# Wq's second half on GpSimd's queue, and the opening of a perceiver kernel put in TensorE's order

## The chip, the core and the metric

The kernel runs on one core of one Trainium2 chip. A core has engines that each work through their own list of instructions in order and wait for one another by semaphores: TensorE (PE, with its weight loads listed as PEld), VectorE (DVE), ScalarE (ACT), GpSimd (POOL) and SyncE (SP), which only issues transfers. Transfers issued by SP, ACT and POOL are carried out by 16 DMA engines that the core's queues share. The metric is the device time of one execution in microseconds (us), lower being better.

## What is computed

Three layers run one after the other on x of 4 x 128 rows by 1024 columns: cross attention to 8192 context rows, causal self attention, and a gated feed-forward layer with 4-bit weights. Each is added to x, and each reads a layernorm of x. What bears on the change is the opening of the first layer:

```python
def _layernorm(x, axis=-1, eps=1e-05):
    m = jnp.mean(x, axis=axis, keepdims=True)
    v = jnp.var(x, axis=axis, keepdims=True)
    return (x - m) / jnp.sqrt(v + eps)
...
    q = (x @ Wq + bq).reshape(1, B * N, H, hd)
    kv = (cond @ Wkv + bkv).reshape(1, -1, 2, H, hd)
...
    q = _fq_sym(q, axis=-1)
    k = _fq_sym(k, axis=-1)
    v = _fq_sym(v, axis=2)
```

Here x is the layernorm of the input, `cond` the context, and `_fq_sym` rounds to 8 bits with a scale for each head (for v, for each column).

## The kernel before

**The opening: queries.** The 512 rows of x are four tiles of 128 rows (`t`). For each tile: x is loaded (`load_x_of_q`, line 259), normalised on DVE with a square root on ACT (`layernorm`, line 132: two statistics of 512 columns, a few tiny operations, and one operation over 1024 columns that writes `xn`), transposed on PE in eight blocks of 128 x 128 into two PSUM tiles (`transposes_of_x`, line 275), copied back by ACT (`copies_of_x`, line 284), and multiplied with Wq. Wq is used in two halves of 512 columns (`n`), each in eight row blocks (`k`) of 128 x 512 that `load_wq` (line 263) fetches. A step of `project_q` (line 289) is one such block against one tile; eight steps make a tile of 128 x 512 queries. PE does all four tiles for the first half, then all four for the second. Eight results of 128 x 512 are then quantised on DVE (`quantise_q`, line 296: add bq, maximum per head, scale, round to 16-bit integers), transposed by DMA from SP's queue (`transpose_q`, line 302) and spread into `qT` by ACT (`store_q`, line 306).

**The opening: weights for values.** Meanwhile the eight row blocks of Wkv for the values come in (`weight_raw`, line 229, 512 KB each) and are split into three parts, so that three matmuls in a reduced format give nearly full precision: a high part on ACT (`weight_hi`), a low part and a difference on DVE (`weight_lo`, lines 158 and 159), and a scaling of the low part on ACT (`weight_up`). The context's tiles of tokens are split in the same way (`load_tokens`, `tokens_hi`, `tokens_lo`), and `project` (line 336, matmuls at line 342) multiplies tokens and weights: 48 matmuls for each of 64 tiles. DVE joins the results (lines 356 and 357), and GpSimd's queue stores them (line 362).

**Buffers.** Wq's blocks share nine buffers (`bufs=NC + 1`). Eight hold the first half and one the first block of the second; block k of the second half takes the buffer of block k-1 of the first, so it cannot be loaded before the last tile has used that one. x's tiles and the tokens' tiles share two buffers (`c_raw`), and so tile 2 of x waits until tile 0 has been normalised, tile 3 until tile 1 has. There is one buffer for `xn`, and two for a raw block of Wkv.

**The order.** The opening's order is written out by hand: `do(step, fn, ...)` puts a call on an agenda (line 219), and `perform` (line 222) makes the calls sorted by `step`, without a scheduler. The numbers are about microseconds, but only their order counts; an engine's list, and a queue's, is what remains of the agenda for it. After the second token tile's first half the order of the value phase is left to a scheduler, up to tile 60 (`V_AUTO`, line 69); from there on it is written by hand again. In the value phase DVE also expands the 4-bit weights of the feed-forward layer, one `expand` (line 386) or two per tile.

**Queues before.** All loads of the opening are on SP's queue, in this order: x 0, Wq's first half with x 1 in between, x 2, x 3, bq, Wq's block 0 of the second half, two blocks of Wkv, and then, each held until its buffer is free, transposes of queries, blocks of Wkv, biases, two token tiles, and the other seven blocks of Wq's second half. GpSimd has nothing between the identity matrix at the start and the first store of values.

Of the kernel before, what the change touches and what calls it, by code (L numbers as in the profile page):

```python
# [41 lines left out]
ALU = mybir.AluOpType  # L42
# [4 lines left out]
P = 128  # L47
B, S, C = 4, 128, 1024
NT = B * S // P
# [37 lines left out]
def tile_perceiver(  # L87
# [26 lines left out]
    nc = tc.nc  # L114
# [14 lines left out]
    gu_d = dram.tile([2 * NI, P, NC, P], F32, name="gu_d")  # L129
    dn_d = dram.tile([2, NI // 2, P, 2, 512], F32, name="dn_d")  # L130

    def layernorm(pool, xt, xn):
        st = pool.tile([P, 2, nc.vector.BN_STATS_DIM], F32, name="ln_st", tag="ln_st", bufs=2)
        for i in range(2):
            nc.vector.bn_stats(st[:, i, :], xt[:, ts(i, 512)])
        mv = pool.tile([P, 2], F32, name="ln_mv", tag="ln_mv", bufs=2)
        nc.vector.bn_aggr(mv, st)
        rstd = pool.tile([P, 1], F32, name="ln_rstd", tag="ln_rstd", bufs=2)
        nc.vector.tensor_scalar_add(rstd, mv[:, 1:2], 1e-5)
        nc.scalar.activation(rstd, rstd, AF.Sqrt)  # L140
        nc.vector.reciprocal(rstd, rstd)
        nc.vector.tensor_scalar(xn, xt, mv[:, 0:1], rstd, ALU.subtract, ALU.mult)

    def split(src, hi, lo, df):

# [60 lines left out]
    q_t = q_s.enter_context(tc.tile_pool(name="q_t", bufs=2, side="right"))  # L206
# [12 lines left out]
    def do(step, fn, *args):  # L219
        agenda.append((step, len(agenda), fn, args))  # L220
# [35 lines left out]
    wq_src = xWq.rearrange("(k p) n -> p k n", p=P)  # L256
    xts, xns, xnTs, qps, qns, wqs, bqs, xpts = {}, {}, {}, {}, {}, {}, {}, {}

    def load_x_of_q(t):
        xts[t] = early.tile([P, C], F32, name=f"xt{t}", tag="c_raw")  # L260
        nc.sync.dma_start(out=xts[t], in_=x[ts(t, P), :])

    def load_wq(n, k):
        wqs[n, k] = q_w.tile([P, 512], F32, name=f"wq{n}_{k}", tag="wq", bufs=NC + 1)
        nc.sync.dma_start(out=wqs[n, k], in_=wq_src[:, k, ts(n, 512)])

    def load_bq():
        bqs[0] = early.tile([P, C], F32, name="bq", tag="c_l2", bufs=1)
# [1 line left out]

    def norm_of_x(t):
        xns[t] = early.tile([P, C], F32, name=f"xn{t}", tag="c_h2", bufs=1)
        layernorm(q_t, xts.pop(t), xns[t])

    def transposes_of_x(t):
        xn = xns.pop(t)
# [93 lines left out]
    shifts = kv_w.tile([P, 2], I32, name="shifts")  # L370
# [66 lines left out]
    def open_pool_of_v():  # L437
        q_s.close()
        pools["v"] = kv_only.enter_context(tc.tile_pool(name="kv_v", bufs=2))

    do(0, load_x_of_q, 0)
    for k in range(NC):
        do(0.1 if k < 3 else 0.3, load_wq, 0, k)
        do(0.6 if k == 0 else 34.6 + 0.88 * k, load_wq, 1, k)
    do(0.2, load_x_of_q, 1)
    for t in range(2, NT):
        do(0.4, load_x_of_q, t)
    do(0.5, load_bq)
    do(32, lambda: nc.sync.dma_start(out=shifts, in_=nibbles))
    do(0.5, nc.vector.memset, vmax, 0.0)  # L450
    for t, at in enumerate((4, 10.5, 20, 22.6)):
        do(at, norm_of_x, t)
        do(9 if t == 0 else 6.85 + 8.15 * t, transposes_of_x, t)
        do(9.1 if t == 0 else 6.95 + 8.15 * t, copies_of_x, t)
        for n in range(2):
            at = (10 + 8.15 * t, 42.6 + 7.05 * t)[n]
            for k in range(NC):
                do(at + 0.88 * k, project_q, n, t, k)
            do(at + 7.2, quantise_q, n, t)
            do(at + 10.7, transpose_q, n, t)  # L460
            do(at + 15, store_q, n, t)
    for k, at in enumerate((28, 30.5, 36.2, 38.7, 44.3, 46.8, 52.4, 54.9)):
        do(20 if k < 2 else at - 8, weight_raw, 1, k)
        do(at - 1.2, weight_hi, 1, k)
        do(at, weight_lo, 1, k)
        do(at + 2.5, weight_up, 1, k)
    for n in range(2):
        do(32, kv_bias, 1, n)
        do(32, load_tokens, n)
    do(58.2, tokens_hi, 0)  # L470
    do(59.4, tokens_lo, 0)
    do(62, load_tokens, 2)
    at = 70.8
    for s in range(2):
        for n in range(2):
            for k in range(NC):
# [163 lines left out]
    for s in range(V_AUTO, 2 * KT):  # L640
        at = TILE * s
# [8 lines left out]
    at = TILE * V_AUTO  # L650
# [11 lines left out]
    at = TILE * (KT - 2)  # L662
# [5 lines left out]
    at = TILE * KT  # L668
# [12 lines left out]
    for u in range(KT):  # L681
        at = TILE * (KT + u)
# [15 lines left out]
    at = TILE * (KT + 2)  # L698
# [4 lines left out]
    first, last = V_QUANT  # L703
    done = 0
    for u in range(first, last):
        at = TILE * (KT + u)
# [5 lines left out]
    at = TILE * (2 * KT - 1)  # L712
# [21 lines left out]
    with tc.tile_pool(name="at_e", bufs=1) as at_e, tc.tile_pool(  # L734
# [245 lines left out]
        with tc.manual_schedule():  # L980
            for s in range(n_steps + LAG_V):
                n, g = divmod(s, NSC)
# [9 lines left out]
                if n < len(units):  # L992
                    h, t = units[n]
# [316 lines left out]
    with tc.manual_schedule():  # L1310
# [10 lines left out]
        for h, (w, n) in enumerate(PARTS):  # L1321
            s = PART * h

            if h > 0:
                for kp in range(NC // 2):
                    at = s + {1: (-28, -24, -13.8, -10), 2: (-35, -31, -6, -3)}.get(h, (-26, -16, -6, -3))[kp]
# [69 lines left out]
        for i in range(2):  # L1396
            at = s - 26 + 10 * i
# [218 lines left out]
```

## Time and profile before

| | us |
|---|---|
| median of 3 runs | 2857.21 (2855.76 to 2858.63) |
| the profiled execution | 2854.13 |
| its span, first to last instruction | 2852.4 |
| PE busy in the span | 2652.6 (93%) |
| DVE busy | 2421.2 (85%) |
| ACT busy | 1267.0 (44%) |
| POOL busy | 455.7 (16%) |

The mean clock granted to TensorE was 0.987 of full speed. The chain of work that ended last goes through PE for 70% of the span and through DVE for 21%; by line, 32% and 16% are the keys-and-values matmuls of line 342, 14% an operation of the attention on DVE (line 789), and 2% the query projection (line 292).

In the rows of a profile, L12 is line 12 of the kernel; `out<-in` names the tiles; `x8` is the number of instructions merged into a row; what stands in brackets is how long the engine was idle just before, and what ended that. SPq is SP's issuing of transfers, whose times are those of issuing and not of moving data. A matmul of 32-bit numbers leaves two records. Rows of one engine can overlap a little, since matmuls are pipelined. DMA transfers end some time after they are issued; the profile gives that time as "to landing".

### The profile page before, as it was taken

The page shows a single profiled execution, that of the slowest core. Times are in us where ns is not written, and L with a number is a line of the kernel's source. Part 1 is how long each engine was busy: PE and PEld are TensorE (multiplying, and loading weights), DVE is VectorE, ACT ScalarE, POOL GpSimd, SP SyncE. Part 2 cuts the span into 40 slices and gives each one's busy share as a digit, 9 for nine tenths or more (in the row PEclk, how much of TensorE's full clock was granted, in tenths as well). Part 3 has the DMA queues.
Part 4 walks back from the last instruction along what each step waited for, and adds up shares of the span by engine and source line. Part 5 has one row for each costly group of instructions (what it writes and reads, how often), then busy time and mean ns, then how long its engine had stood idle before and what let it go on. Part 6 is the DMA issues. An engine that isn't in the chain of part 4 may idle for free.

```text
span 2852.4 us, 41096 instructions
## 1 busy us (share of the span) xinstructions
PE 2652.6 (93%) x15496; PEld 2059.5 (72%) x15496; DVE 2421.2 (85%) x3960; ACT 1267.0 (44%) x1404; POOL 455.7 (16%) x608
## 2 busy tenths in 40 slices
PE   8999999999999999999996777787778899999998
PEld 3788888888878888888884555555555777788886
DVE  6899999555699998888879999999997898876674
ACT  4211211112323333333217999999994244333332
POOL 0011111000012222222113332233312000000000
PEclk9999999999999999999998999999999999999999
DMA  5555565222447777777536888877875222122222
GB/s 188 170 200 201 194 212 207 104 96 95 146 106 198 192 192 186 188 186 191 130 88 144 164 167 165 154 149 161 164 145 153 76 83 67 52 96 96 94 92 96
DMA packets 450631, 412.66 MB, mean 145 GB/s; under 512 B 354872, under 2 KB 359544, under 8 KB 450432
## 3 DMA queue, kind: packets, MB, share of 16 engines
q1 hardware_dynamic: 402848, 251.70, 36.3%
q0 software_dynamic: 46528, 157.29, 17.2%
q8 instruction: 122, 2.00, 0.3%
q10 hardware_dynamic: 1056, 1.05, 0.2%
q14 instruction: 77, 0.63, 0.1%
HBM read 220.14 MB, written 104.34 MB: 114 GB/s over the span
## 4 chain that ended last, share of the span: by engine, by line
PE 70%; DVE 21%; issue 4%; POOL 2%; ACT 1%; DMA 1%; DVEq 0%; ACTq 0%
PE kv_a L342 32%; PE kv_b L342 16%; DVE e L789 14%; PE acc_a L1130 3%; PE up_a L165 3%; PE gate_a L165 3%; PE y_a L1503 3%; POOL sk L762 2%; PE q_ps L292 2%; PE acc_b L1130 1%; PE up_b L165 1%; PE gate_b L165 1%; PE y_b L1503 1%; PE a_pt L832 1%; DVE sw_l L158 1%
## 5 line engine op out<-in xcount | busy, mean ns | idle before, releaser
L342 PE MATMUL kv_b<-w_d,c_d 128*128 128x512 f32 x2048 | 806.0, 394 | 0.3 <-DVE c_d L159 0.3
L342 PE MATMUL kv_a<-w_h,c_h 128*128 128x512 f32 x2048 | 806.3, 394 | 0.0
L342 PE MATMUL kv_a<-w_l,c_l 128*128 128x512 f32 x2048 | 806.0, 394 | 0.2 <-ACT w_l L246 0.2
L789 DVE CUSTOM_DVE_ANT_0 e<-sc,sk 128x1024 f32<-128x1024 f32 x512 | 593.0, 1220 | 8.1 <-PE sc L782 7.0
L817 ACT ACTIVATE a<-e,m,sqs 128x4096 int16<-128x4096 f32 x128 | 486.9, 3804 | 24.1 <-DVE m L806 23.8
L342 PEld LDWEIGHTS kv_a<-w_l,c_l 128*128 128x128 f32 x2048 | 384.8, 188 | 89.6 <-ACT w_l L246 0.6
L342 PEld LDWEIGHTS kv_b<-w_d,c_d 128*128 128x128 f32 x2048 | 384.8, 188 | 89.5 <-DVE c_d L159 0.8
L342 PEld LDWEIGHTS kv_a<-w_h,c_h 128*128 128x128 f32 x2048 | 384.9, 188 | 88.8 <-issue 0.2
L155 ACT ACTIVATE c_h<-c_raw 128x1024 fp32r<-128x1024 f32 x128 | 135.2, 1057 | 418.9 <-PE kv_a L342 404.6
L356 DVE SCALAR_TENSOR_TENSOR f<-kv_a,bkv 128x512 f32<-128x512 f32 x256 | 175.8, 687 | 163.4 <-PE kv_a L342 162.8
L782 PE MATMUL sc<-kt,qT 64*128 64x512 bf16 x1024 | 205.5, 393 | 104.9 <-DVE mx L789 100.8
L581 ACT CAST kst<-kT 128x512 bf16<-128x512 int16 x128 | 89.4, 699 | 302.3 <-DMA kT<-ki 302.3
L832 PE MATMUL a_pt<-ident,a 128*128 128x128 f32 x1024 | 174.3, 295 | 21.1 <-ACT a L817 16.4
L357 DVE SCALAR_TENSOR_TENSOR f<-kv_b,f 128x512 f32<-128x512 f32 x256 | 176.7, 690 | 20.3 <-DVE f L356 0.9
L762 POOL PARTITION_BROADCAST sk<-sk_row x120 | 142.3, 1297 | 312.3 <-DVE mx L789 312.2
L832 PEld LDWEIGHTS a_pt<-ident,a 128*128 128x128 f32 x1024 | 111.4, 144 | 86.9 <-ACT a L817 48.9
L782 PEld LDWEIGHTS <-qT 64*128 64x128 bf16 x1024 | 75.3, 93 | 132.7 <-issue 102.7
L158 DVE TENSOR_TENSOR fw_l<-fw_raw,fw_h 128x1024 fp32r<-128x1024 f32 x64 | 78.3, 1224 | 99.4 <-ACT fw_h L155 99.3
L158 DVE TENSOR_TENSOR c_l<-c_raw,c_h 128x1024 fp32r<-128x1024 f32 x128 | 155.7, 1217 | 5.8 <-ACT c_h L155 5.6
L159 DVE SCALAR_TENSOR_TENSOR c_d<-c_l,c_raw 128x1024 fp32r<-128x1024 f32 x128 | 156.3, 1221 | 2.3
L155 ACT ACTIVATE fw_h<-fw_raw 128x1024 fp32r<-128x1024 f32 x64 | 67.8, 1060 | 175.4 <-PE y_a L1503 71.6
L548 ACT CAST vq<-vi 128x1024 f16<-128x1024 int16 x64 | 67.0, 1046 | 171.0 <-DVE vi L541 123.9
(211 smaller groups left out, 4104.9 us busy)
## 6 DMA issues: line engine op xcount, KB each, us to landing
c_raw<-in_ctxT SPq DMA_DIRECT2D x128, 512.0 KB, 3.6
v_d<-f POOLq DMA_DIRECT2D x64, 512.0 KB, 3.1
vl<-v_d POOLq DMA_DIRECT2D x64, 512.0 KB, 4.2
gu_d<-w_ffn POOLq DMA_DIRECT2D x44, 512.0 KB, 3.1
fw_raw<-gu_d SPq DMA_DIRECT2D x42, 512.0 KB, 3.2
k_d<-kst POOLq DMA_DIRECT2D x128, 128.0 KB, 3.5
vq_d<-vq POOLq DMA_DIRECT2D x32, 512.0 KB, 5.2
kt<-k_d SPq DMA_DIRECT2D x64, 256.0 KB, 3.5
```

What stands on the lines that cost most here:

```text
L155: nc.scalar.mul(hi, src, 1.0 - 0.5 / UP)
L158: nc.vector.tensor_tensor(lo, src, hi, ALU.subtract)
L159: nc.vector.scalar_tensor_tensor(df, lo, -1.0 - UP, src, ALU.mult, ALU.add)
L165: nc.tensor.matmul(ps, lhsT=lhs(i, k), rhs=rhs(i, k), start=(k == 0 and i != 1), stop=(k == NC - 1 and i != 0),)
L342: nc.tensor.matmul(ps, lhsT=tokens[s][i][:, k, :], rhs=w3[s < KT][k][i][:, ts(n, 512)], start=(k == 0 and i != 1), stop=(k == NC - 1 and i ...
L356: nc.vector.scalar_tensor_tensor(f, a, 1.0 + 1.0 / UP, bias[s < KT][n], ALU.mult, ALU.add)
L357: nc.vector.scalar_tensor_tensor(f, b, -1.0 / UP, f, ALU.mult, ALU.add)
L762: nc.gpsimd.partition_broadcast(tile_of_scales(h, g), sks_at[h][32 * c : 32 * c + 1, ts(half, SC)], channels=P)
L782: nc.tensor.matmul(ps[:, ts(i, 512)], lhsT=qT[rows, h, ts(t, P)], rhs=kts[h, g // 2][rows, ts(g % 2, 512)], start=True, stop=True,)
L789: nc.vector.tensor_tensor_reduce(out=state[n]["e"][-1][:, ts(g % (NSC // NEC), SC)], in0=ps, in1=sks_at[h, g], scale=1.0, scalar=LOWEST, o ...
L817: nc.scalar.activation(a, st["e"][c], AF.Exp, bias=st["m"], scale=sqs[:, 0, t, h : h + 1], accum_out=sums[h][:, t, c : c + 1],)
L832: nc.tensor.transpose(pt[:, i, :], a[:, at_word + P * i : at_word + P * i + P], ident)
```

## The change

`load_x_of_q` fetches tile 0 of x in two halves of 512 columns, and `layernorm` writes tile 0's `xn` in two operations of 512 columns. `load_wq` puts blocks 1 to 7 of the second half on GpSimd's queue instead of SP's. The agenda's numbers are new: two blocks of Wkv and bq move ahead of tiles 2 and 3 of x on SP's queue, the first two token tiles are loaded earlier, the biases later; PE takes seven steps of a tile, and not six, before the next tile's transposes; the layernorms, splits and quantisations are placed anew on DVE, with a quantisation no longer ahead of the next layernorm but behind it; ACT's conversions follow. The numbers of instructions stay, but for one more load of x and one more operation on DVE. With the hand-written part, the scheduler's order of DVE, ACT, POOL and SP in the value phase differs too, up to about its end; PE's list is the same from the second half of the queries on.

```diff
-    def layernorm(pool, xt, xn):
+    def layernorm(pool, xt, xn, parts=1):
...
-        nc.vector.tensor_scalar(xn, xt, mv[:, 0:1], rstd, ALU.subtract, ALU.mult)
+        for i in range(parts):
+            cols = ts(i, C // parts)
+            nc.vector.tensor_scalar(
+                xn[:, cols], xt[:, cols], mv[:, 0:1], rstd, ALU.subtract, ALU.mult
+            )
...
-        nc.sync.dma_start(out=xts[t], in_=x[ts(t, P), :])
+        for i in range(2 if t == 0 else 1):
+            cols = ts(i, 512) if t == 0 else slice(0, C)
+            nc.sync.dma_start(out=xts[t][:, cols], in_=x[ts(t, P), cols])
...
-        nc.sync.dma_start(out=wqs[n, k], in_=wq_src[:, k, ts(n, 512)])
+        queue = nc.gpsimd if n == 1 and k > 0 else nc.sync
+        queue.dma_start(out=wqs[n, k], in_=wq_src[:, k, ts(n, 512)])
...
-        layernorm(q_t, xts.pop(t), xns[t])
+        layernorm(q_t, xts.pop(t), xns[t], parts=2 if t == 0 else 1)
...
     do(0, load_x_of_q, 0)
     for k in range(NC):
         do(0.1 if k < 3 else 0.3, load_wq, 0, k)
-        do(0.6 if k == 0 else 34.6 + 0.88 * k, load_wq, 1, k)
+        do(0.65 if k == 0 else 30, load_wq, 1, k)
     do(0.2, load_x_of_q, 1)
-    for t in range(2, NT):
-        do(0.4, load_x_of_q, t)
-    do(0.5, load_bq)
-    do(32, lambda: nc.sync.dma_start(out=shifts, in_=nibbles))
+    do(0.45, load_bq)
+    do(0.5, load_x_of_q, 2)
+    do(0.55, load_x_of_q, 3)
     do(0.5, nc.vector.memset, vmax, 0.0)
-    for t, at in enumerate((4, 10.5, 20, 22.6)):
+    first = [8.1 + 8.05 * t for t in range(NT)]
+    second = [39.2 + 7.03 * t for t in range(NT)]
+    for t, at in enumerate((4, 9, 16.4, 24.5)):
         do(at, norm_of_x, t)
-        do(9 if t == 0 else 6.85 + 8.15 * t, transposes_of_x, t)
-        do(9.1 if t == 0 else 6.95 + 8.15 * t, copies_of_x, t)
-        for n in range(2):
-            at = (10 + 8.15 * t, 42.6 + 7.05 * t)[n]
+        at = first[t] - (1.6 if t == 0 else 1.9)
+        do(at, transposes_of_x, t)
+        do(at + 0.1, copies_of_x, t)
+        for n, q_at in enumerate(((19, 27.5, 33, 40.9)[t], (48.7, 54.1, 61, 67.5)[t])):
             for k in range(NC):
-                do(at + 0.88 * k, project_q, n, t, k)
-            do(at + 7.2, quantise_q, n, t)
-            do(at + 10.7, transpose_q, n, t)
-            do(at + 15, store_q, n, t)
-    for k, at in enumerate((28, 30.5, 36.2, 38.7, 44.3, 46.8, 52.4, 54.9)):
-        do(20 if k < 2 else at - 8, weight_raw, 1, k)
-        do(at - 1.2, weight_hi, 1, k)
-        do(at, weight_lo, 1, k)
-        do(at + 2.5, weight_up, 1, k)
+                do((first, second)[n][t] + 0.88 * k, project_q, n, t, k)
+            do(q_at, quantise_q, n, t)
+            do(q_at + 3.1, transpose_q, n, t)
+            do(q_at + 8.5, store_q, n, t)
+    for k, (raw, hi, lo) in enumerate(
+        (
+            (0.4, 12.8, 13),
+            (0.6, 19.5, 22),
+            (16.5, 24, 30.4),
+            (24.6, 34, 36),
+            (33, 37.5, 38.4),
+            (38.5, 42, 43.8),
+            (41, 49.5, 51.6),
+            (46.3, 55, 57),
+        )
+    ):
+        do(raw, weight_raw, 1, k)
+        do(hi, weight_hi, 1, k)
+        do(lo, weight_lo, 1, k)
+        do(lo + 2.6, weight_up, 1, k)
     for n in range(2):
-        do(32, kv_bias, 1, n)
-        do(32, load_tokens, n)
-    do(58.2, tokens_hi, 0)
-    do(59.4, tokens_lo, 0)
-    do(62, load_tokens, 2)
-    at = 70.8
+        do(27.6, load_tokens, n)
+        do(40, kv_bias, 1, n)
+    do(45, tokens_hi, 0)
+    do(46.2, tokens_lo, 0)
+    do(48.8, load_tokens, 2)
+    do(60, lambda: nc.sync.dma_start(out=shifts, in_=nibbles))
+    at = 67.4
```

## The prediction

> **What bounds it now.** I read the chain of waits first. Its shares by line say that TensorE's matmuls are the path: the projections of lines 342 and 292, then DVE in the attention. The change touches only the opening, so next came the busy time of 100 us stretches, to see whether a gain there survives. After the stretch come the columns its length, then busy time (instructions) of PE, PEld, DVE, ACT, POOL, then granted clock, DMA share, GB/s.
>
> ```profile
> 0.00:100.00 100.00, 87.31 (x263) 48.64 (x264) 66.32 (x126) 38.79 (x51) 1.42 (x7) 0.97 0.58 175
> 100.00:200.00 100.00, 100.00 (x434) 81.26 (x433) 100.00 (x220) 19.13 (x18) 14.32 (x25) 1.00 0.55 195
> ...
> 300.00:400.00 100.00, 100.00 (x434) 81.26 (x433) 98.61 (x196) 19.13 (x18) 16.42 (x26) 1.00 0.56 198
> ...
> 1200.00:1300.00 100.00, 100.00 (x434) 81.24 (x433) 89.78 (x139) 34.67 (x39) 22.31 (x34) 1.00 0.74 190
> ```
>
> PE misses 12.7 us in the first 100 us (7.88 before it begins, 0.85 and 3.96 below) and next to nothing until 1400 us. What starts earlier there shifts all that follows. So the question is where those 12.7 us lie. The timeline of PE over the opening answers it (start, length, operation, idle before it in brackets):
>
> ```profile
> 7.88 1.94 PE L281 MATMUL pt<-ident,xn 128*128 128x128 f32 x8 [7.88 <-DVE xn L142]
> 9.64 6.27 PE L292 MATMUL q_ps<-wq,xnT 128*128 128x512 f32 x12
> 15.75 1.04 PE L281 MATMUL pt<-ident,xn 128*128 128x128 f32 x8
> 16.62 7.03 PE L292 MATMUL q_ps<-wq,xnT 128*128 128x512 f32 x16
> 24.50 1.09 PE L281 MATMUL pt<-ident,xn 128*128 128x128 f32 x8 [0.85 <-DVE xn L142]
> 25.43 7.03 PE L292 MATMUL q_ps<-wq,xnT 128*128 128x512 f32 x16
> 32.30 1.04 PE L281 MATMUL pt<-ident,xn 128*128 128x128 f32 x8
> 33.18 9.61 PE L292 MATMUL q_ps<-wq,xnT 128*128 128x512 f32 x22
> 46.74 29.84 PE L292 MATMUL q_ps<-wq,xnT 128*128 128x512 f32 x62 [3.96 <-DMA wq<-in_xWq]
> 76.01 0.80 PE L342 MATMUL kv_a<-w_h,c_h 128*128 128x512 f32 x1
> ```
>
> A projection step is two records. Eight steps take 25.43 to 32.30, so 0.859 us each; a tile's eight transposes take 15.75 to 16.62, 0.87. From 16.62 there are 58 steps and two sets of transposes to the first keys-and-values matmul: 58 x 0.859 + 1.74 = 51.6, which would end at 68.2. It comes at 76.01, so 7.8 us are lost: 0.85 for xn of the third tile, 3.95 (42.79 to 46.74) for the second half of Wq, 2.64 after it (31 steps need 26.63, from 46.74 to 76.01 are 29.27), and 0.4 in small seams. The 2.64 are a slow clock and short waits:
>
> ```profile
> 44.00:48.00 4.00, 1.26 (x2) 0.50 (x2) 3.35 (x8) 1.06 (x1) 0.00 (x0) 0.69 1.19 312
> 48.00:52.00 4.00, 3.99 (x5) 1.46 (x5) 0.34 (x1) 2.42 (x4) 0.00 (x0) 0.50 0.97 341
> 52.00:56.00 4.00, 4.00 (x10) 1.71 (x9) 3.93 (x4) 1.98 (x2) 0.00 (x0) 0.96 0.51 173
> ```
>
> After the idle stretch TensorE was granted half its clock until about 52 us. Why did Wq come late? SP's queue:
>
> ```profile
> 36.53 1.53 SPq L323 DMA_DIRECT2D c_raw<-in_ctxT  x1
> ...
> 38.58 0.43 SPq L323 DMA_DIRECT2D c_raw<-in_ctxT  x1
> 39.11 0.37 SPq L265 DMA_DIRECT2D wq<-in_xWq  x1
> ```
>
> The load takes the buffer of Wq step 0, which tile 3 releases at 33.18 + 3 x 0.859 = 35.8. It is issued at 39.11, behind loads of Wkv, a transpose, two biases and two token tiles, and its matmul starts at 46.74: 3.3 us in the queue, 7.6 in transfers that share the engines with 1.5 MB issued just ahead.
>
> **The change, part by part.**
>
> Seven Wq loads go to GpSimd's queue. Nothing stands ahead of them there but the identity's making (over at 1.5 us), nothing behind but the first store of values, which is due after the first keys-and-values tile. Each waits for PE alone. With tile 3's step 0 done at 33.9 (below), the loads are released every 0.859 us, and load j is needed 6.9 us after its release, because seven more steps of tile 3 and one of the new half lie between. The trace of before has no Wq load on this queue. Nearest row: loads of vl from DRAM there, twice the size, 0.55 us to issue and 3.5/4.2/6.8 us to landing (min/median/max). At 4.2 from issue there are 2.7 us to spare, at 6.8 still 0.1. The low end, a smaller landing, changes nothing; the high end is 7.6 us, what Wq took on the crowded queue: 0.7 late. I take 4.2: the two token tiles that crowded it are issued by about 28 us here, and the biases after the sixth Wkv load, at about 39.
>
> Here a rule speaks against the change. The Trainium skill, "SBUF — State Buffer", section "SBUF: two separate sides", says that a transfer from GpSimd's queue has its descriptors written by GpSimd, which is locked out while DVE runs an operation in a two-port mode; its subsection "A bandwidth-pool intuition that's wrong (but worth ruling out)" prices one such case at 3100 ns instead of 620. By the rule, if every load met it, the seven would be generated at 3.1 us each: load 7 issued at 33.9 + 21.7 = 55.6, landed about 59, needed at 45.9, so 13 us of stall. By the row: while DVE is busy 100% (100 to 200 us), POOL issues its stores in 0.53 to 0.77 us, and stores of v_d land in 3.2. In the 8 us in question DVE runs quantisations and splits (1.22 us for 1024 columns, two inputs), not the 0.81 us normalisation, which looks like the fast mode and ends by 28 us. I take the row.
>
> SP loses those seven issues (0.33 to 0.95 us each, off its way), so Wkv's loads leave as soon as their buffers free. The 1 KB load of shifts moves behind them all; its user comes far later. The first two Wkv tiles move to the start of the queue, one of them and bq ahead of tiles 2 and 3 of x. By bytes: x 0.5, Wq 2.1, x 0.5, Wkv 0.5, bq 0.5, x 1.0 MB. The trace moved 0.84 MB by 5 us and 344 GB/s up to 9; continued at 370 that lands Wkv at 13, bq at 14.5, tile 2 of x at 16, tile 3 (held for its buffer to 12.6) at 18. ACT converts the first Wkv tile ahead of tile 1's copies, so a landing after 16 would hold up PE; there are 3 us between.
>
> DVE's order. With a layernorm of 3.0, a quantisation of 3.0 and a split of 2.45 us (sums of their rows), and PE as the pace: norm 1 to 12.6, split 0 to 16.5, norm 2 to 19.6 (PE wants it at 23.4; before it came at 24.45, behind a quantisation that waited for PE), quantisation to 22.6, split 1 to 25.1, norm 3 to 28.1 (wanted at 31.2). Five more quantisations, six splits of weights and one of tokens follow; the last weight is ready at 60.3, tokens at 49, and the keys need them at 67. DVE then waits for PE. The 0.85 goes, and no new wait takes its place: slack is 3 us at the norms, 7 at the weights. The quantisations' order does hold up ACT's stores and with them splits 4 to 7 (ACT waits for the transpose by DMA, 4.2 us), which is in these figures.
>
> The first norm by halves. x lands at 4.70 and two statistics of 0.68 follow. With two loads the first half should land about a microsecond earlier, and its statistics (0.64 by start-to-start) hide under the second's landing; 0 if the second half lands that much later (one issue later is 0.46), so 0.2 to 0.64. The 0.81 normalisation becomes two of about 0.44, and PE begins after the first: 0.37; DVE pays 0.07 more. I take 0.64 + 0.37 = 1.0, at worst 0.5. PE's cold start (1.94 for the first transposes, against 1.04) stays.
>
> Scheduler. From the second token tile to the 60th, DVE's work is placed by a scheduler, and it is placed otherwise now, with nearly the same instructions. Per token tile PE needs 11.2 us. Summing DVE's rows between successive token splits in the new order gives at most 14.1 in one tile and a backlog of 2.9 us at worst (before: 11.9 and 0.7), against a lead of about one tile. Cost nothing, at most 2.9.
>
> **Sum.** 7.8 + 1.0 = 8.8; without the seams 0.85 + 3.95 + 2.64 + 1.0 = 8.4. I take 8.6: keys and values start at 67.4, not 76.0. The profiled execution took 2854.13 (span 2852.4 and 1.7 around it), which becomes 2845.5. It lies 3.1 under the median of the three runs, 2857.21; for a median I say **2848.6 us**.
>
> **Rivals.** (1) The loads land some microseconds late: biases, Wkv and Wq meet in the engines from 39 us on, as they met before. A landing of 7.6 plus one re-cooled clock costs 0.7 + 2.6; up to 4 us of stall and the clock give 6.6. Time 2852 to 2855. For: the DMA share is 0.97 to 1.19 in that stretch of before. Against: the token tiles are out of it. Chance 0.12. (2) Slower: GpSimd's generation of descriptors is the pace. For a period of p us load 7 lands at 33.9 + 7p + 3.6 and is due at 45.9; the stall, 7p - 8.4, begins at p = 1.2, and with the clock's 2.6 it eats the whole gain at p = 2.06. At the rule's 3.1 it is 13.3 + 2.6 = 15.9, a time of 2864. Against it: 0.53 to 0.77 in every row of POOL. Chance 0.08. (3) The opening gains, and the other order of DVE gives part back: 2.9 us of backlog met twice is 5.8, time 2851 to 2855. Against: the lead of a tile. Chance 0.06. The main case has 0.74, with 2846 to 2851 of its own.
>
> **Range and chances.** A measurement of this kernel tells a change from none at about 0.2%, 5.7 us. The main case is faster by more; of rival 1 a quarter. Faster 0.77, same 0.15, slower 0.08. The range is 2844 (PE's floor, and medians that wander by 1.5) to 2854 (most of rivals 1 and 3).
>
> **What would show it.** PE's first row near 6.9; no idle before the rows of line 292 (now 301), clock 1.00 from about 12 us on; first kv_a near 67.4; wq on POOL issued every 0.86 us from 34. Wrong if PE waits for wq or ACT's xnT, or if PE busy falls under 99 between 100 and 700 us.

## The result, and the profile after

The changed kernel took 2847.41 us (median of 7 runs, 2844.23 to 2852.84) against 2857.21 (7 runs) for the kernel before: a ratio of 0.9965, 95% interval 0.9955 to 0.9974. Measured again on another chip, beside its two halves, it was 2850.28 against 2857.1, 0.9976 (0.9968 to 0.9984). By these two medians it is faster by 0.24% to 0.35%. The profiled execution took 2847.28, its span 2845.4.

The busy time of the first 100 us of the changed kernel (columns as before):

```profile
0.00:100.00 100.00, 92.58 (x294) 53.97 (x295) 78.83 (x148) 39.19 (x52) 6.81 (x17) 1.00 0.64 197
100.00:200.00 100.00, 100.00 (x434) 81.25 (x433) 100.00 (x228) 19.13 (x18) 14.37 (x25) 1.00 0.56 200
```

TensorE works 5.3 us more of them, and after 100 us it is full, as before. The timeline of PE shows where the gain is:

```profile
6.75 1.94 PE L290 MATMUL pt<-ident,xn 128*128 128x128 f32 x8 [6.75 <-DVE xn L144]
8.52 7.77 PE L301 MATMUL q_ps<-wq,xnT 128*128 128x512 f32 x14
16.13 1.04 PE L290 MATMUL pt<-ident,xn 128*128 128x128 f32 x8
...
23.87 1.04 PE L290 MATMUL pt<-ident,xn 128*128 128x128 f32 x8
...
32.49 14.45 PE L301 MATMUL q_ps<-wq,xnT 128*128 128x512 f32 x32
47.58 21.73 PE L301 MATMUL q_ps<-wq,xnT 128*128 128x512 f32 x50 [0.64 <-DMA wq<-in_xWq]
68.74 0.80 PE L351 MATMUL kv_a<-w_h,c_h 128*128 128x512 f32 x1
```

The wait for xn at tile 2 is gone, and of the 3.96 us for Wq 0.64 is left. Keys and values start at 68.74 instead of 76.01, 7.27 earlier. The first score matmul of the attention comes at 1496.5 instead of 1504.3 and the last at 2134.36 instead of 2141.55: what was gained in the opening is carried to the end of that stage, 7.2 of it.

The clock stays at full speed, in the stretches that showed half of it before:

```profile
44.00:48.00 4.00, 3.34 (x7) 0.89 (x6) 1.49 (x6) 1.99 (x3) 0.00 (x0) 1.00 1.04 393
48.00:52.00 4.00, 4.00 (x11) 1.74 (x10) 3.59 (x4) 2.40 (x4) 0.00 (x0) 1.00 0.55 165
```

The loads themselves are not quick, though. The chain of waits of this stretch (start, length, what):

```profile
32.65 6.88 PE q_ps L301 x16
39.53 0.28 issue
39.82 7.71 DMA wq<-in_xWq
```

The last Wq block leaves 0.28 us after the step that frees its buffer, and then takes 7.71 us to land, as long as the block on SP's queue before (7.6). What was saved is time in the queue: the first of these blocks leaves at 34.69 us, where it left at 39.11 before. The experiments show that the new order alone saves it as well.

### The profile page after: what moved, and what is told of

The parts are those of the page before. It is cut to its first block, busy times and chain, and to the rows that moved or that the text cites. A ratio compares the mean times of both kernels' runs of the same rounds, so it can differ in the third digit from the quotient of the medians.

```text
span 2845.4 us, 41117 instructions
## 1 busy us (share of the span) xinstructions
PE 2655.8 (93%) x15496; PEld 2062.3 (72%) x15496; DVE 2421.7 (85%) x3961; ACT 1266.1 (44%) x1404; POOL 461.8 (16%) x615
## 4 chain that ended last, share of the span: by engine, by line
PE 71%; DVE 21%; issue 4%; POOL 2%; ACT 1%; DMA 1%; DVEq 0%; SPq 0%; ACTq 0%; POOLq 0%
PE kv_a L351 33%; PE kv_b L351 17%; DVE e L812 14%; PE up_a L169 3%; PE gate_a L169 3%; PE y_a L1526 3%; PE acc_a L1153 2%; PE q_ps L301 2%; POOL sk L785 2%; PE gate_b L169 1%; PE up_b L169 1%; PE y_b L1526 1%; PE acc_b L1153 1%; PE a_pt L855 1%; DVE sw_l L162 1%
## 5 line engine op out<-in xcount | busy, mean ns | idle before, releaser
L855 PE MATMUL a_pt<-ident,a 128*128 128x128 f32 x1024 | 176.3, 297 | 21.5 <-ACT a L840 15.3
```

Source lines behind the costliest of these rows:

```text
L855: nc.tensor.transpose(pt[:, i, :], a[:, at_word + P * i : at_word + P * i + P], ident)
```

## The experiments

Seven questions, answered by twelve runs of nine kernels: the changed one and eight edits. Whole times of single runs scatter by several us, above all in the attention: from its first to its last score matmul the fourteen profiles take 637.3 to 643.6 us. So the opening is compared by landmarks of the traces, and whole times only where a kernel was timed over many executions. In this table "loss" is the time from the first projection step behind tile 3's transposes to the first keys-and-values matmul, above the 34.79 us that it takes where PE does not wait (the sixth experiment), less 0.86 for the one step more that lies between in the old order. "Longest Wq landing" is the longest time from issue to landing of blocks 1 to 7 of Wq's second half; where they are on SP's queue, it is read from the last update of each load's semaphore in the trace, since the profile's view gives only one of the seven. "A step sooner" means that PE takes six steps, not seven, before tile 1's transposes.

| kernel | PE's first transposes | tile 1's transposes | keys and values start | loss | longest Wq landing | first score matmul |
|---|---|---|---|---|---|---|
| before | 7.88 | 15.75 (a step sooner) | 76.01 | 7.18 | 7.6 | 1504.3 |
| changed | 6.75 | 16.13 | 68.74 | 1.46 | 7.7 | 1496.5 |
| changed, again | 6.89 | 16.80 | 70.24 | 2.29 | 8.5 | 1498.0 |
| queue alone | 7.55 | 16.00 (a step sooner) | 73.72 | 4.65 | 10.9 | 1503.1 |
| queue alone, again | 7.60 | 16.60 (a step sooner) | 72.85 | 3.18 | 9.4 | 1503.9 |
| order alone | 6.64 | 15.96 | 67.70 | 0.59 | 5.9 | 1495.4 |
| order alone, again | 6.57 | 15.28 | 67.67 | 1.24 | 6.4 | 1495.5 |
| x whole | 7.78 | 17.55 | 70.72 | 2.02 | 8.3 | 1498.5 |
| warmed | 6.85 | 14.30 | 67.08 | 1.63 | 7.9 | 1496.0 |
| biases later | 6.91 | 16.32 | 69.60 | 2.14 | 8.4 | 1497.6 |
| extra DVE work | 6.69 | 15.74 | 66.89 | 0 | 5.0 | 1494.6 |
| SP, warmed, biases later | 7.00 | 14.45 | 67.25 | 1.65 | 5.9 | 1494.9 |
| GpSimd, warmed, biases later | 6.85 | 14.41 | 66.33 | 0.44 | 6.7 | 1494.2 |
| the same, again | 6.53 | 13.98 | 66.22 | 0.98 | 7.2 | 1494.0 |

**1 and 2. Is it the queue or the order?** The kernel before with the new queue alone:

```diff
-        nc.sync.dma_start(out=wqs[n, k], in_=wq_src[:, k, ts(n, 512)])
+        queue = nc.gpsimd if n == 1 and k > 0 else nc.sync
+        queue.dma_start(out=wqs[n, k], in_=wq_src[:, k, ts(n, 512)])
```

> The kernel before, with one edit: blocks 1 to 7 of Wq's second half are loaded from GpSimd's queue; order and first norm as before. If the queue is what freed TensorE: the loads are issued from about 35.8 us (when tile 3 releases the buffers) every 0.86 us and land 5 to 6 us later, so the 3.95 us of idle and the 2.64 of slow clock go but the 0.85 wait for xn stays; keys and values start at 69.4 to 70.5 us, against 76.0 before and 68.7 after. If the order did it, by taking two token tiles and two biases (1.5 MB) out of the way: these still share the DMA engines from 36 us, the loads land 7.5 to 10 us after issue, TensorE idles 1 to 3 us there and its clock falls again; start at 72 to 75.

And the changed kernel with those loads back on SP, at the moment of their release (it keeps all the rest of the change, the first norm by halves too):

```diff
-        queue = nc.gpsimd if n == 1 and k > 0 else nc.sync
+        queue = nc.sync
...
-        do(0.65 if k == 0 else 30, load_wq, 1, k)
+        do(0.65 if k == 0 else 32.5 + 0.88 * k, load_wq, 1, k)
```

> The changed kernel with the seven Wq loads back on SP's queue, placed there at the time their buffers come free. If the queue is what matters: they stand behind a transpose and a Wkv load, and two of them behind the transpose of tile 2's queries, which waits for DVE until 37 us; the last ones land 1 to 3 us later than after the change, keys and values start at 70 to 72 us. If the order is what matters: SP's list is nearly clear there, the start is within 0.5 us of the 68.7 after the change.

The queue alone brings the keys and values 2.3 us forward, to 73.72 as in the second case, and leaves 4.65 us of loss, though the clock stays at 1.00: its blocks leave at once but take up to 10.9 us to land among the token tiles, and PE waits for them again and again:

```profile
44.05 3.54 PE L293 MATMUL q_ps<-wq,xnT 128*128 128x512 f32 x6 [1.03 <-DMA wq<-in_xWq]
...
52.56 21.73 PE L293 MATMUL q_ps<-wq,xnT 128*128 128x512 f32 x50 [0.88 <-DMA wq<-in_xWq]
```

The order alone brings them forward by 8.31, more than the whole change, and beyond the half microsecond around 68.7 that was expected. PE and SP's issues there:

```profile
46.54 21.73 PE L301 MATMUL q_ps<-wq,xnT 128*128 128x512 f32 x50 [0.32 <-DMA wq<-in_xWq]
67.70 0.80 PE L351 MATMUL kv_a<-w_h,c_h 128*128 128x512 f32 x1
```

```profile
34.98 2.16 SPq L274 DMA_DIRECT2D wq<-in_xWq  x4
37.45 1.20 SPq L313 DMA_TRANSPOSE qnT<-qn  x1
38.74 1.00 SPq L274 DMA_DIRECT2D wq<-in_xWq  x2
```

The first block leaves at 34.98, as early as on GpSimd's queue (34.69), and the seven land 5.2 to 5.9 us after issue. That this is because one queue keeps what is issued later behind Wq is likely, but no run shows it by itself. Both were then timed over many executions on one chip, with the changed kernel.

> The changed kernel itself, on one chip with its two halves and the warmed version, so that whole times can be set side by side. By the start of the keys and values (68.74 in its trace, 76.01 before) it is 7.3 below before: 0.9974. The first measurement gave 9.8 below (0.9965), of which 2.5 has no place in the two traces. Theory: that is spread of the attention stage, and here the ratio is 0.997 to 0.9978. Rival: something later than the first 70 us gains too, and the ratio is again 0.9965 or less.

> The changed kernel with the second half of Wq on SP. Theory (the order is what gains, the queue nothing): keys and values start at 67 to 69, ratio within 0.0005 of the changed kernel's. Rival (the queue is a part of the gain): 1 us or more above the changed kernel.

> The kernel before with the second half of Wq on GpSimd's queue and nothing else. By its first trace keys and values start 2.3 earlier than before (73.72): ratio 0.999 to 0.9995. If the queue alone made the change, it would be 0.9975.

| one chip | median | ratio to before | 95% interval |
|---|---|---|---|
| before | 2857.1 | | |
| changed | 2850.28 | 0.9976 | 0.9968 to 0.9984 |
| order alone | 2849.05 | 0.9973 | 0.9965 to 0.998 |
| queue alone | 2856.18 | 0.9996 | 0.9988 to 1.0004 |

So the gain is the order's, which here means SP's list, the engines' lists and the first norm by halves together; the queue adds nothing that can be told from none. No run changed SP's list alone. The first measurement's 9.8 us, 2 us more than the 7.8 between the first score matmuls, did not come again, so it was spread. The queue alone keeps little of its earlier start: 1.2 of 2.3 us at the first score matmul in its first trace, and 0.4 of 3.16 in its second, where keys and values start at 72.85. The timeline of PE in the second shows where the first part goes:

```profile
72.85 0.80 PE L343 MATMUL kv_a<-w_h,c_h 128*128 128x512 f32 x1
73.97 0.51 PE L343 MATMUL kv_a<-w_l,c_l 128*128 128x512 f32 x1 [0.32 <-DVE c_l L158]
75.32 0.47 PE L343 MATMUL kv_b<-w_d,c_d 128*128 128x512 f32 x1 [0.85 <-DVE c_d L159]
```

The second keys-and-values matmul comes 1.12 after the first, the third 1.35 after that (0.64 and 0.23 in the changed kernel): TensorE arrives before the old DVE order has split the tokens, and 1.6 us go there. A wait of 1.3 us for DVE at the scales of a later key tile (line 601) takes most of the rest.

**3. What is the first norm by halves worth?** Tile 0 of x whole, the rest as changed:

```diff
-        for i in range(2 if t == 0 else 1):
-            cols = ts(i, 512) if t == 0 else slice(0, C)
+        for i in range(1):
+            cols = slice(0, C)
...
-        layernorm(q_t, xts.pop(t), xns[t], parts=2 if t == 0 else 1)
+        layernorm(q_t, xts.pop(t), xns[t], parts=1)
```

> The changed kernel with tile 0 of x loaded whole and normalised in one operation. TensorE begins about 1.1 us later (7.9, not 6.75). Theory that the full clock comes at nearly the same moment whenever TensorE begins (11.5 us before, 11.8 after): most of the earlier start was spent at half clock, keys and values start at 69.2, only 0.5 later. Rival, that an earlier start moves everything: 69.9, a full 1.1 later.

PE starts 1.03 later and tile 1's transposes come 1.42 later than in the first trace of the changed kernel, 0.75 later than in its second. Keys and values start at 70.72, later than both 69.2 and 69.9, so neither expectation was met. The difference is the cold clock: weight loads of the projection come 0.85 apart at first and 0.43 apart, the spacing of full speed, from 11.84 us on in the changed kernel, 12.94 in its second trace, 13.69 here, 11.46 before. (The rows print a clock of 1.00 for this stretch as well, because each trace's first clock record, at 11.58, 12.79, 13.38 and 11.39, begins only there.) That moment scatters by more than a microsecond in one and the same kernel, so no pair of traces prices the halves. The table does it better, over its ten cold traces. Add 0.86 where tile 1's transposes come a step sooner: with tile 0 whole (before, queue alone twice, x whole) they come at 16.6 to 17.6, 17.1 on average; with halves (changed twice, order alone twice, biases later, extra DVE work) at 15.3 to 16.8, 16.0 on average. PE itself starts 1.0 earlier on average, and full speed comes 1.2 earlier (11.6 against 12.8). So the earlier start is kept in full as far as these averages tell, though the two groups overlap; the theory of a fixed moment is not borne out.

**4. Is the cold clock the rest?** Twelve matmuls of the identity with itself ahead of the first transposes, their result unused:

```diff
+    def warm_up(n):
+        pt = kv_ps.tile([P, 4, P], F32, name="warm", tag="ps")
+        for i in range(n):
+            nc.tensor.matmul(pt[:, i % 4, :], lhsT=ident, rhs=ident, start=True, stop=True)
...
+    do(0.05, warm_up, 12)
```

> The changed kernel with 12 matmuls of the identity with itself (128x128) on TensorE before the first transposes, into a PSUM tile that nothing reads; the result is unchanged. If the half clock at the start comes from TensorE having been idle: these take 0.43 us each at half clock from about 1.6 us on, the full clock is there before the first transposes, which take 1.04 and not 1.94 us, and the first steps 0.86 us; keys and values start 2 to 2.6 us earlier, at 66 to 66.7, unless Wq's second half, which is late in the engines anyway, takes some of it back. If the clock follows something else: no earlier, 68.7 to 69.2.

```profile
1.57 5.49 PE L287 MATMUL warm<-ident 128*128 128x128 f32 x24 [1.57 <-POOL ident masks.py:199]
6.85 1.09 PE L295 MATMUL pt<-ident,xn 128*128 128x128 f32 x8
8.18 6.28 PE L306 MATMUL q_ps<-wq,xnT 128*128 128x512 f32 x14 [0.24 <-ACT xnT L301]
14.30 1.04 PE L295 MATMUL pt<-ident,xn 128*128 128x128 f32 x8
```

Against the first trace of the changed kernel, the first transposes take 1.09 instead of 1.94, the 14 records of the first steps 6.28 instead of 7.77, and tile 1 begins 1.83 us sooner. The start of keys and values keeps 1.66 of it. So the cold clock costs about 1.8 us of its own, a little less than the 2 to 2.6 expected; the loss behind tile 3 (1.63) stays.

**5. Do the biases slow the Wq blocks?**

```diff
-        do(40, kv_bias, 1, n)
+        do(50, kv_bias, 1, n)
```

> The changed kernel with one due time changed: the two loads of the bias of the keys and values (bkv, 256 KB each) go out on SP after the last Wkv tiles but one and a tile of the context, not at 40 us among the Wq loads. Theory (the last Wq block took 7.7 us to land, against 4.2 in the prediction, because the bkv loads and a Wkv tile share the DMA engines with it): its landing falls to about 6, the wait at 47.58 (0.64) mostly goes and so do the slow records of weight loads before it (0.85 and 0.82): keys and values start at 67.5 to 67.9 instead of 68.74. Rival (GpSimd's own pace or its descriptors make the landing long): landing stays at 7.5 or more and the start at 68.7. Single time within the spread of runs of the changed kernel, so no verdict from it.

No: with the two bias loads at 54 us the longest landing is 8.4 and the loss 2.14, between what the changed kernel shows in its two traces. The theory fell.

**6. Does DVE hold up GpSimd's descriptors?** Eight instructions of the fast kind on DVE, in the very stretch:

```diff
+    for i in range(8):
+        do((32.95, 33.05)[i // 4], nc.vector.tensor_scalar_add, vmax, vmax, 0.0)
```

> The changed kernel with eight extra VectorE instructions that add 0.0 in place to a float32 tile of 128x1024 (vmax, still zero), four before and four behind the quantisation of query tile 2: they run at about 34 to 42 us, where GpSimd issues the seven Wq loads. By the Trainium skill's page on SBUF an instruction of this kind (float32, SBUF to SBUF, one input) can take the port pair that GpSimd needs to write descriptors: the rule makes the GpSimd issues wait for it, so an issue of 0.54 us becomes about 1.2 to 3, some of them start late, and the last loads land 2 us or more later (keys and values start at 70 or more). The row of the changed kernel (issues of 0.54 us beside a VectorE that was busy with two-input instructions, 0.74 for one) makes no difference: issues 0.54 to 0.74, start 68.4 to 69.2. Either way VectorE's later work moves back by about 5 us, which its slack takes.

Timelines of DVE (the extra instructions) and of GpSimd's issues in this kernel:

```profile
33.49 2.87 DVE L228 TENSOR_SCALAR vmax<-vmax 128x1024 f32<-128x1024 f32 x4
...
39.18 2.87 DVE L228 TENSOR_SCALAR vmax<-vmax 128x1024 f32<-128x1024 f32 x4
```

```profile
34.30 1.46 POOL L274 DMA_DIRECT2D wq<-in_xWq  x2 [32.79 <-PE q_ps L301]
...
39.43 0.55 POOL L274 DMA_DIRECT2D wq<-in_xWq  x1 [0.32 <-PE q_ps L301]
```

The first two loads and the last are issued inside DVE's fast stretches, in the times they have without them (1.41 for two, 0.54 for one). No lock shows, so the rule's case (70 or more) fell, and the other (68.4 to 69.2) fell too, on the early side. The surprise is the landing, which the view of the tile wq gives, first for the changed kernel, then with the extra work:

```profile
DMA to landing us min/median/max: 5.4/5.9/7.7
```

```profile
DMA to landing us min/median/max: 4.2/4.7/5.0
```

With more work on DVE no block is late, PE has no wait left (this is the trace that the loss is counted from), and keys and values start at 66.89, 1.85 earlier than in the changed kernel. What moved is what DVE's later results set off. The transfers from 40 to 42 us (queue 0 is GpSimd's, queue 1 SP's; packets, MB, and their time as a share of the 16 engines), changed and then with the extra work:

```profile
q0 software_dynamic: 125, 0.39, 88.9%
q1 hardware_dynamic: 437, 0.11, 44.3%
```

```profile
q0 software_dynamic: 192, 0.63, 98.4%
q1 hardware_dynamic: 5, 0.00, 0.3%
```

The 437 packets with 0.11 MB between them are a transpose of queries by DMA (`transpose_q`: 544 packets, 0.13 MB in all). While it is carried out the Wq queue moves 0.39 MB in 2 us at nearly the same busy share, and 0.25 in the next two; the extra work put the transpose behind 42 us, and Wq moved 0.63 MB. In the changed kernel's second trace Wq moved 0.30 MB from 40 to 44 us, and in the five other traces of the new order with Wq on GpSimd and no extra work its queue falls below 0.1 MB in some microsecond between 40 and 44, beside or just behind a transpose. SP's Wkv block and biases, issued at 39.69 and 40.07, move next to no bytes before 44 us in the changed kernel, which fits that moving the biases did nothing. That it is the transpose, and not the Wkv block or the biases which moved with it, rests on these rows of one trace; no kernel moved the transpose alone. Nor does every load beside a transpose slow down: in the kernel with extra work the transpose is carried out from 42 us on, and Wq's last 0.21 MB move in that first microsecond.

**7. The pieces together.** The changed kernel with the warm-up of experiment 4 and the biases of experiment 5, with Wq on SP as in experiment 2 or left on GpSimd:

> The changed kernel with three edits that earlier runs speak for: the second half of Wq goes out on SP in the order of release, the loads of bkv go out behind it, and twelve matmuls on the identity run on TensorE ahead of the first transposes. Theory (what is left of the loss is the cold clock, 2.3 us, and about 1 us of waits for Wq that the transfers of bkv make): the first projection steps take 0.86, tile 1's transposes start near 14.3, no wait for Wq above 0.3, keys and values start at 65.5 to 66.3 against 68.74, and the median is 2.5 to 3 below the changed kernel: ratio to before near 0.9955. Rival (once everything runs 1.8 us earlier, Wq is late by as much as TensorE is early): start near 67.1 as with the warm-up alone, ratio 0.996 to 0.9965.

> As the run before, with the second half of Wq left on GpSimd. If the queue itself is worth something (GpSimd issues the moment a slot is released, while SP's order puts a store's transpose and a Wkv tile between), keys and values start 0.3 to 1 us earlier than with SP. If only the bytes that share the DMA engines count, the two start within 0.3 us of each other. If GpSimd's path is the slower one in itself, this start is later by 0.5 to 1 us (as the order alone on SP started 1.04 earlier than the changed kernel).

They took 2851.1 (16 runs, ratio 0.9977, 0.9969 to 0.9984) and 2851.48 (12 runs, 0.9976, 0.9967 to 0.9984). Neither reached the hoped-for 0.9955, nor even the rival's 0.9965. With TensorE 1.7 us earlier, SP's order seems to cost: its first Wq block left at 34.91, behind a transpose and a Wkv block, when GpSimd's had left at 33.30, and keys and values start 0.92 later, at 67.25 where the rival had 67.1. One trace of each shows this, and the totals do not tell the two apart. The one on GpSimd ran again beside the changed kernel:

> The changed kernel with the bias loads behind Wq and twelve matmuls ahead of the first transposes, again, beside the changed kernel. By the starts (66.33 against 68.74) it is 2.4 below the changed kernel. Its first measurement (0.9976) is above the changed kernel's first (0.9965), on another chip. Theory: the chips differ in the attention stage, and here it is 1.5 to 3 below the changed kernel. Rival: the full-speed start is given back later, where the clock is throttled, and it is level with the changed kernel or above.

2849.29 (14 runs, 0.9973, 0.9965 to 0.9981) against 2850.28: one microsecond, within the intervals, although in the two traces its keys and values start 4.0 sooner and its first score matmul too. From there to the last score matmul its profile takes 643.6 us, against 638.1. Much of this is the chance of single profiles: its profiled run lies 1.9 us above the median of its kernel, the changed kernel's 1.6 below. The first profile of the same kernel took 640.2 there, the changed kernel's first 637.9, the kernel before 637.3, and order alone 642.9 and 641.1. Whether part of an earlier start is also given back in the attention, these runs leave open. No version beats the changed kernel by more than the measurement can tell.

## Why the prediction was right, step by step

**The bound.** Right. PE stays full from 100 to 700 us, and the lead won in the opening is still there at the last score matmul (7.2 us).

**The sum.** Right in kind, a little large. Predicted: keys and values at 67.4, a profile of 2845.5, a gain of 8.6. Measured: 68.74 (70.24 in the second trace), a profile of 2847.28, which is 6.85 below the one before, and medians 9.8 and 6.8 apart. That the first median came within 1.2 us of the 2848.6 forecast is partly luck: 2 us of its gain have no place in the traces and did not come again. The 7.27 of the trace is 0.9 for xn, 5.72 for Wq and its clock (losses of 7.18 and 1.46), 0.48 at the start and 0.17 in seams. The loss before was a little larger than the 7.8 of the prediction: where PE does not wait, 41 steps take 34.79 (0.849 each, not 0.859), which leaves 8.4. The step that was mis-sized is the landing: "At 4.2 from issue there are 2.7 us to spare"; it was 5.4 to 7.7, and 3.9 to 8.5 in the second trace, beyond the 7.6 of the crowded queue that the text took as its high end. By its own sign ("Wrong if PE waits for wq") this step failed, with waits of 0.64 us and, in the second trace, 0.63 and 0.85. The reason given for the low end, that the token tiles and then the biases were out of the way, missed the transpose of queries on SP's queue, if the rows of experiment 6 are read rightly.

**Halves.** "I take 0.64 + 0.37 = 1.0": PE does start 1.13 earlier, or 0.89 to 1.03 against x whole. Only 0.48 is left of it at tile 1 in the two traces of the result, but 1.1 on the average of the ten cold traces (experiment 3), so the size looks right. "PE's cold start (1.94 for the first transposes, against 1.04) stays" was priced by the first transposes alone: the slow clock also covers the first steps, and the moment at which it ends, 10.1 to 13.7 us in these ten, scatters more than the gain.

**GpSimd's descriptors.** Right: the row was taken, not the rule. Issues are 0.54 to 0.74 us in every kernel with Wq on GpSimd, and experiment 6 put the fast instructions of the rule (the Trainium skill, "SBUF — State Buffer", section "SBUF: two separate sides") beside them without effect. That those were in a two-port mode is inferred from 0.69 us for 1024 columns, where operations with two inputs take 1.22.

**DVE's order and the scheduler.** The xn wait is gone in every kernel with the new order, and nothing replaces it (with the warm-up, PE waits 0.2 to 0.4 us for xnT or xn at the start). The prediction's walk through DVE's work ran ahead of the truth by up to 4.2 us (the last weight's split ends at 63.8, not 60.3; the tokens' at 53.2, not 49), which the slack took. The backlog in the value phase cost nothing: from the first keys-and-values matmul to the first score matmul the changed kernel takes 1427.8 us, the kernel before 1428.3.

**Rivals.** The first one's late landings were there, but not through the biases (experiment 5) and without its clock effect: landings of up to 8.5 us left single waits of PE below 1 us, and after them the clock stayed at 1.00. What the prediction did not see is how the change divides. Its first and largest term, Wq's 3.95 and the clock's 2.64, it gave above all to the move to GpSimd's queue. The queue alone gives 0.9 us in whole time, which cannot be told from none, and the order alone 8.05. The move was needless for the gain that it was to bring.

## What to carry to other kernels

When a load is late, look at what stands ahead of it and at what moves beside it, before giving it a queue of its own: here, a new order of the whole opening gave all of the gain with one queue, and a second queue under the old order only let the late block leave early and land late. An engine that is made to wait less in the opening gains little if the next stage's inputs are not ready for it, as the new queue under the old order shows. Compare small changes by landmarks of the traces as well as by totals, and take a second trace: the same kernel's opening differed by 1.5 us between two.

## What was not expected of the hardware

A transpose by DMA of 0.13 MB, 544 packets, coincides with the slowest stretch of the loads on the other queue: 0.10 MB in each of the two microseconds from 41 us on in the changed kernel, where 0.30 and 0.32 MB are moved in the two from 40 us on in the kernel with extra DVE work. That it is the cause is not shown.

TensorE's clock fell to 0.50 in the 4.78 us for which the weight loads stood still before, and not at all in the stands of up to 1.9 us in the other kernels. At the start of the ten cold traces, full speed comes 3.6 to 6.1 us after the first transposes begin, and differs by 1 to 1.5 us between two executions of one kernel. Twelve matmuls on the identity, begun at 1.57 us, remove that start from the path in all four traces that have them.
